# Causal attention: the values' product after every unit of scores, in banks of its own, summed by GpSimd

## The chip, the cores and the metric

The kernel runs on one core of a Trainium2 chip. The metric is device microseconds from start to end of one execution; the median of three runs of the kernel before is 4479.21 us (4477.16 to 4482.08). TensorE is called PE in the profile, VectorE DVE, ScalarE ACT, GpSimd POOL and SyncE SP.

## The reference, cut to what matters

The program is a chain of layers on x of 2 batches x 2048 tokens x 256 features in fp32: a mixture of experts, an attention without a mask, the experts again, a recurrent layer, a causal attention, the recurrent layer again. The change lies in the causal attention:

```python
q, k, v = shape(x @ w_q.T), shape(x @ w_k.T), shape(x @ w_v.T)   # 16 heads of 16
q, k = rotary(q), rotary(k)
q = q / sqrt(DIM_PER_HEAD)
scores = einsum('bhqd,bhkd->bhqk', q, k) + einsum('bhqd,qkd->bhqk', q, rel)
scores = where(causal, scores, NEG_INF)
attn = softmax(scores, axis=-1)
ctx = einsum('bhqk,bhkd->bhqd', attn, v) + einsum('bhqk,qkd->bhqd', attn, rel)
out = ctx.transpose(0, 2, 1, 3).reshape(B, L, MODEL_DIM) @ w_o.T
```

rel depends on the distance of query and key alone, clipped at 32. So only a band of 32 keys before each query needs more than a constant.

## The kernel before, in words

Both attentions work on groups: one batch, one block of 512 queries, four of the 16 heads (J = 4), each head's 16 features in a strip of 32 partitions. Scores are computed twice. The first pass (`largest`) puts queries on the partitions of a PSUM bank, and DVE takes each row's maximum. The maximum is transposed and added into a spare row of the queries (`subtract`), so that the second pass (`exponential`, in the causal attention `exp_band`, `exp_far` and `exp`) has keys on the partitions and maxima already subtracted; ACT writes its exponentials to SBUF (`pT`). The values' product (`weighted`) takes these, 128 keys at a time, four heads side by side in the columns of the array. One column of the values is ones, so that the sums for the division come with it. `divide` transposes the group's result and divides.

The order of PE, ACT and DVE is that of the program, written out by hand: the kernel counts steps, and each step has two units of score work. A unit is one block of 128 keys of the second pass for one group, and one piece of the first pass for a later group, four heads each. Other work (projections, rotation, positions, division, outputs) is entered under a step by `at(step, ...)`. The order of POOL and SP is left to a scheduler. Two fp32 matmul records of the profile make one product.

In the first attention (`attention0`, L606 on) half of a step's other work and then the values of the unit before follow each unit. Each key block's values go to a bank of their own; ACT copies it to SBUF (L673, L676), and POOL adds it to the group's result there (L677).

In the causal attention (`attention1`) a step's two units come one after the other, then all of the step's other work, then the values of both units of the step before. They accumulate in one PSUM bank per group, `z.acc[t]`, from the first key block to the positions' product (L1103), after which `z.take` copies it out (L553). Blocks on the diagonal take only the columns from q0 on. The band of a diagonal block comes by DMA from DRAM, is added to on POOL (L999), and is transposed into the scores' bank by PE (L1056, L1060). `rotate` (L885 to L894) makes rotated keys and queries: a copy on ACT, a shuffle on DVE, three or four operations on POOL. `by_position` (L923) is the first to read the rotated queries on PE. `ln_stats` puts the normalisation of later blocks on POOL (L100, L102, L113).

The pool of PSUM has eight banks for all of it. A causal group of query block qc has 4 (qc + 1) key blocks; over both batches there are 32 groups and 320 key blocks.

Of the kernel before, what the change touches and what calls it, by code (L numbers as in the profile page):

```python
# [10 lines left out]
F32 = mybir.dt.float32  # L11
AF = mybir.ActivationFunctionType
ALU = mybir.AluOpType
# [4 lines left out]
P = 128  # L18
# [7 lines left out]
TB = 512  # L26
NTB = NT // TB
CPB = TB // P
# [5 lines left out]
J = 4  # L34
# [8 lines left out]
def macaron_kernel(ctx: ExitStack, tc: tile.TileContext, t: dict, out: bass.AP):  # L43
    nc = tc.nc
# [26 lines left out]
    def bank():  # L71
        return psum.tile([P, TB], F32, name="s")
# [12 lines left out]
    class Norm:  # L85


        def __init__(self):
            self.mv, self.rstd, self.xn, self.xnT = {}, {}, {}, {}
# [42 lines left out]
    def rows(j):  # L132
        return slice(32 * j, 32 * j + 32)
# [351 lines left out]
    class Pieces:  # L485


        def __init__(self, s, name, norm, weights_o, bias):
            self.keep = pool(s, name + "_keep")
            self.wk = pool(s, name + "_wk", 2)  # L490
            self.norm, self.wo, self.bias = norm, weights_o, bias
            self.mnegs = []
            for n in range(2):
                m = self.keep.tile([P, CPB, J, 32], F32, name=f"mneg{n}")
                nc.gpsimd.memset(m, 0.0)
                self.mnegs.append(m)
            self.cn, self.cT, self.o, self.acc, self.pTs, self.q = ({} for _ in range(6))

        def ln_stats(self, b, qc):
            blk = b * SB + qc  # L500
# [46 lines left out]
                )  # L547
            nc.vector.tensor_tensor(self.q[t], self.q[t], pm, ALU.add)  # L548

        def take(self, t):  # L550

            self.o[t] = self.wk.tile([P, TB], F32, name="o")
            nc.scalar.copy(self.o[t], self.acc.pop(t))  # L553

        def divide(self, t, b, qc, g, own):
            if (b, qc) not in self.cn:
# [45 lines left out]
    def attention0(norm, tail, wq, wk_, wv, wo, bff):  # L602
# [7 lines left out]
        with ExitStack() as s:  # L610
            z = Pieces(s, "a0", norm, wo, bff)
            kpool = pool(s, "a0_k", side="right")
            vpool = pool(s, "a0_v", side="right")
            wk, q = z.wk, z.q
            groups = [(b, qc, g) for b in range(B) for qc in range(SB) for g in range(G)]
            NG = len(groups)
# [45 lines left out]
            def weighted(t, kb):  # L662
                b, qc, g = groups[t]
                pv = bank()
                for j in range(J):
                    h = (g % 2) * J + j
                    nc.tensor.matmul(  # L667
                        pv[rows(j), :], lhsT=v[b, g // 2][:, kb, ds(h * VW, 32)],
                        rhs=z.pTs.pop((t, kb, j)), start=True, stop=True,
                    )  # L670
                if kb == 0:
                    z.o[t] = wk.tile([P, TB], F32, name="o")
                    nc.scalar.copy(z.o[t], pv)  # L673
                else:
                    part = wk.tile([P, TB], F32, name="part", bufs=4)
                    nc.scalar.copy(part, pv)  # L676
                    nc.gpsimd.tensor_tensor(z.o[t], z.o[t], part, ALU.add)  # L677

            jobs = Jobs()
            at = jobs.at  # L680
# [29 lines left out]
            for step in range(min(jobs), max(jobs) + 1):  # L710
                todo = jobs.get(step, [])
                for n in range(2):
                    te, tm = (step - 9) // PER, step // PER
                    ke, um = ((step - 9) % PER) * 2 + n, (step % PER) * 2 + n
                    exps = 0 <= te < NG
# [144 lines left out]
    def attention1(norm, tail, w, relk, relv, kbias, dramp, skew):  # L860
# [4 lines left out]
        with ExitStack() as s:  # L865
            z = Pieces(s, "a1", norm, w["o"], None)
            wk, q = z.wk, z.q
            groups = []
# [3 lines left out]
            NG = len(groups)  # L872
            kT, v, mx, band, cos, sin, wb, wT, st, pd, lead = ({} for _ in range(11))
# [156 lines left out]
            def exp_far(t, kb, j):  # L1030
                b, qc, g = groups[t]
                qb = kb - qc * CPB
                ps = exp_bank(t, kb, j)
                k = kT[b, kb // CPB, g][rows(j), ts(kb % CPB, P)]
                q0 = 0
                if qb >= -1:
                    q0 = (qb + 1) * P
                    if q0 < TB:
                        nc.tensor.matmul(  # L1039
                            ps[0 : P - BAND, ds(q0, P)], lhsT=k[:, 0 : P - BAND],  # L1040
                            rhs=q[t][rows(j), ds(q0, P)], start=True, stop=True,
                            skip_group_check=True,
                        )
                    q0 += P
                if q0 < TB:
                    nc.tensor.matmul(  # L1046
                        ps[:, q0:], lhsT=k, rhs=q[t][rows(j), q0:], start=True, stop=True,
                        skip_group_check=True,
                    )

            def exp_band(t, kb, j):
                b, qc, g = groups[t]
                qb = kb - qc * CPB
                ps = exp_bank(t, kb, j)
                if qb >= 0:
                    nc.tensor.transpose(ps[:, ts(qb, P)], band[t][:, qb, j, BAND:], ident)  # L1056
                if qb + 1 < CPB:


                    nc.tensor.transpose(  # L1060
                        ps[:, ts(qb + 1, P)], lead[t][:, ds(((qb + 1) * J + j) * BW, P)], ident
                    )

            def exp(t, kb, j):
                q0 = max(0, kb - groups[t][1] * CPB) * P
                z.pTs[t, kb, j] = wk.tile([P, TB], F32, name="pT", bufs=16)
                nc.scalar.activation(z.pTs[t, kb, j][:, q0:], st.pop((t, kb, j))[:, q0:], AF.Exp)  # L1067

            def weighted(t, n, kb):
                b, qc, g = groups[t]  # L1070
                q0 = max(0, kb - qc * CPB) * P
                if n == 0:
                    z.acc[t] = bank()
                for j in range(J):
                    h = (g % 2) * J + j
                    nc.tensor.matmul(  # L1076
                        z.acc[t][rows(j), q0:],
                        lhsT=v[b, kb // CPB, g // 2][:, kb % CPB, ds(h * VW, 32)],
                        rhs=z.pTs.pop((t, kb, j))[:, q0:], start=n == 0, stop=False,
                        skip_group_check=True,  # L1080
                    )

            def positions_load(t):
                wb[t] = wk.tile([P, CPB, J * BAND], F32, name="s2", bufs=4)
# [15 lines left out]
                nc.vector.tensor_copy(wT[t], pw)  # L1100

            def positions(t):
                nc.tensor.matmul(  # L1103
                    z.acc[t], lhsT=relv, rhs=wT[t], start=False, stop=True, skip_group_check=True
                )


            Ms, Me, Es, Ee, Rs = [], [], [], [], []
            for n, (b, qc, g) in enumerate(groups):
                size = 2 * (qc + 1)  # L1110
                start = Me[-1] + 1 if n else 0
                if n > 1:
                    start = max(start, min(Ee[n - 2] + 1, Es[n - 2] + 5) + 2 - (size - 2))
                if n > 3:
                    start = max(start, Ee[n - 4] + 4)
                Ms.append(start)
                Me.append(start + size - 1)
                start = Me[-1] + 2
# [2 lines left out]
                Es.append(start)  # L1121
                Ee.append(start + size - 1)
                Rs.append(start + (3 if size == 2 else 4))
            largest_at, exp_at, weighted_at = Jobs(), Jobs(), Jobs()
            for n, (b, qc, g) in enumerate(groups):
                for i, piece in enumerate(pieces(qc)):
                    largest_at.at(Ms[n] + i // 2, None, n, *piece)
                for i, kb in enumerate(key_blocks(qc)):
                    exp_at.at(Es[n] + i // 2, None, n, i, kb)
                    weighted_at.at(Es[n] + i // 2 + 1, None, n, i, kb)  # L1130
            jobs = Jobs()
            at = jobs.at
            index = {x_: n for n, x_ in enumerate(groups)}
# [27 lines left out]

            for step, fn, *args in tail:
                at(Me[-1] + step, fn, *args)
            if True:
                for step in range(min(jobs), max(jobs) + 1):
                    exps = [a for _, a in exp_at.get(step, ())]
                    maxs = [a for _, a in largest_at.get(step, ())]
                    late = []
                    for n in range(2):
                        e = exps[n] if n < len(exps) else None  # L1170
                        m = maxs[n] if n < len(maxs) else None
                        qb = e[2] - groups[e[0]][1] * CPB if e is not None else -2
                        if -1 <= qb < CPB - 1:
                            for j in range(J):
                                exp_band(e[0], e[2], j)
                        for j in range(J):
                            if e is not None:
                                exp_far(e[0], e[2], j)
                                if qb == CPB - 1:
                                    late.append((e[0], e[2], j))  # L1180
                                else:
                                    exp(e[0], e[2], j)
                            if m is not None:
                                largest(*m, (j + 2) % J if e is not None else j)
                    for a_ in late:
                        exp_band(*a_)
                        exp(*a_)
                    jobs.run(step)
                    for _, a_ in weighted_at.get(step, ()):
                        weighted(*a_)  # L1190
                    for n in range(NG):
                        if step == max(Rs[n], Ee[n] + 1):
                            z.take(n)


    def load_all(stack, pool_, names):
# [210 lines left out]
```

## Time and profile before

| what | value |
|---|---|
| median of the runs | 4479.21 us |
| profiled execution, its own time | 4366.3 us |
| its span, first to last instruction | 4364.5 us |
| mean granted PE clock | 0.985 |
| causal attention, about | 2740 to 4180 us of the span |
| busy there (of 1440 us) | PE 1408.28, DVE 869.91, ACT 696.91, POOL 479.93 |
| first attention, about | 560 to 2090 us of the span |

The profile is of one execution, whose own time is below the median of the runs. A row of it names line, engine and operation; a matmul's duration is modelled, and several run at once in strips of the array, so that a busy PE isn't one at its full pace. The starts of matmuls show the pace.

### The profile page before, as it was taken

Reading aid. Unit: us, or ns where it says so; the run is one execution under the profiler, and the core shown is the slowest. Engines: PE = TensorE matmul, PEld = TensorE weight load, DVE = VectorE, ACT = ScalarE, POOL = GpSimd, SP = SyncE. Lnnn points to the kernel's source line nnn. Section 1 sums busy time; section 2 is a strip of 40 time slices with the busy share of each in tenths; the row PEclk is TensorE's granted clock in tenths of the full one; section 3 lists DMA queues with packets and bytes.
Section 4 is the critical chain, followed back from the end, with each engine's and each line's share of the span. In section 5 each row is a group of like instructions: output and inputs, shape, how many; then the busy total and the mean of one; then the engine's idle time right before and its main releaser. Section 6 shows DMA issues by size and latency. Waiting matters only on the chain.

```text
span 4364.5 us, 76072 instructions
## 1 busy us (share of the span) xinstructions
PE 4211.6 (96%) x28512; PEld 2106.7 (48%) x28512; DVE 2703.6 (62%) x6176; ACT 2398.1 (55%) x4835; POOL 1480.3 (34%) x1374
## 2 busy tenths in 40 slices
PE   7998999999999999999999897999999999999999
PEld 4664333333334333333356544565555555655545
DVE  6245787877766878888543343566666455666533
ACT  2331788877777888888623231344545534454532
POOL 4253333345332333333352311542222444322100
PEclk9999999999999999999999998999999999999999
DMA  7331000000000000000334200453212345222101
GB/s 250 122 116 42 1 1 1 1 1 1 1 1 2 1 1 1 1 1 8 110 131 126 84 10 22 105 117 81 66 44 49 73 100 114 58 61 45 44 21 39
DMA packets 355503, 224.33 MB, mean 51 GB/s; under 512 B 146496, under 2 KB 338496, under 8 KB 355136
## 3 DMA queue, kind: packets, MB, share of 16 engines
q1 hardware_dynamic: 342848, 185.89, 16.3%
q0 software_dynamic: 12288, 33.57, 2.4%
q8 instruction: 227, 3.72, 0.4%
q14 instruction: 140, 1.15, 0.1%
HBM read 114.29 MB, written 105.12 MB: 50 GB/s over the span
## 4 chain that ended last, share of the span: by engine, by line
PE 87%; DVE 6%; issue 2%; POOL 2%; DMA 1%; ACT 1%; SPq 0%; POOLq 0%; ACTq 0%; DVEq 0%
PE s L655 13%; PE s L667 11%; PE s L138 11%; PE s L643 10%; PE s L961 8%; PE s L1046 6%; PE s L358 6%; PE s L1076 6%; PE s L377 3%; PE s L585 1%; PE s L1056 1%; PE s L526 1%; PE s L1039 1%; PE s L1060 1%; DVE mx L969 1%
## 5 line engine op out<-in xcount | busy, mean ns | idle before, releaser
L647 DVE TENSOR_REDUCE mx<-s 128x1 f32<-128x512 f32 x2048 | 1271.5, 683 | 363.7 <-PE s L643 362.9
L660 ACT ACTIVATE pT<-s 128x512 f32<-128x512 f32 x2048 | 1064.2, 618 | 206.8 <-PE s L643 202.4
L655 PE MATMUL s<-q,kT 32*128 32x512 f32 x4096 | 1016.5, 616 | 6.3 <-DVE q L548 5.4
L643 PE MATMUL s<-kT,q 32*128 32x512 f32 x4096 | 1015.2, 618 | 6.8 <-DVE mx L647 5.5
L677 POOL TENSOR_TENSOR o<-o,part 128x512 f32<-128x512 f32 x480 | 608.4, 1268 | 1101.6 <-ACT part L676 1100.6
L1067 ACT ACTIVATE pT<-s 128x512 f32<-128x512 f32 (+3 forms) x1280 | 592.8, 545 | 485.6 <-PE s L1046 293.6
L655 PEld LDWEIGHTS s<-q,kT 32*128 32x128 f32 x4096 | 414.4, 184 | 471.9 <-DVE mx L647 310.5
L969 DVE TENSOR_REDUCE mx<-s 128x1 f32<-128x512 f32 (+1 forms) x768 | 466.5, 677 | 246.6 <-PE s L961 226.8
L667 PE MATMUL s<-pT,v 128*32 128x512 f32 x4096 | 549.9, 605 | 2.0 <-DVE mx L647 1.9
L643 PEld LDWEIGHTS s<-kT,q 32*128 32x128 f32 x4096 | 405.3, 184 | 138.0 <-ACT pT L660 71.6
L961 PE MATMUL s<-kT,q 32*128 32x160 f32 (+7 forms) x2240 | 398.1, 441 | 0.0
L676 ACT COPY part<-s 128x512 f32<-128x512 f32 x480 | 296.9, 619 | 79.3 <-PE s L667 78.8
L358 PE MATMUL s<-we,xT 128*128 x592 | 278.9, 593 | 0.6 <-ACT xT L353 0.6
L961 PE MATMUL s<-b,q 32*128 32x512 f32 (+7 forms) x1280 | 271.0, 528 | 6.2 <-POOL b L894 5.7
L1046 PE MATMUL s<-q,kT 32*128 32x512 f32 (+3 forms) x1152 | 265.4, 510 | 1.6 <-DVE s L1100 1.6
L1076 PE MATMUL s<-pT,v 128*32 128x512 f32 (+3 forms) x2560 | 266.7, 534 | 0.0
L999 POOL TENSOR_TENSOR band<-band,mneg 128x640 f32<-128x640 f32 x128 | 160.8, 1260 | 309.8 <-DVE mneg L995 309.4
L961 PEld LDWEIGHTS s<-kT,q 32*128 32x128 f32 x2240 | 226.1, 186 | 61.1 <-DVE mx L969 17.6
L1046 PE MATMUL s<-q,b 32*128 32x512 f32 (+3 forms) x896 | 248.4, 566 | 0.0
L667 PEld LDWEIGHTS s<-pT,v 128*32 128x32 f32 x4096 | 82.2, 108 | 337.6 <-ACT pT L660 282.0
L365 DVE TENSOR_TENSOR h<-sg,s 128x256 f32<-128x256 f32 x148 | 62.3, 421 | 288.5 <-ACT sg L363 288.5
L985 DVE CUSTOM_DVE_ANT_0 band<-s,band 128x160 f32<-128x160 f32 (+1 forms) x512 | 155.2, 315 | 95.4 <-PE s L1046 51.6
(209 smaller groups left out, 5535.2 us busy)
## 6 DMA issues: line engine op xcount, KB each, us to landing
band<-skew SPq DMA_DIRECT2D x32, 1280.0 KB
pd<-band SPq DMA_DIRECT2D x32, 1280.0 KB, 8.3
xs<-places SPq DMA_DIRECT2D x148, 128.0 KB, 2.1
results<-y SPq DMA_DIRECT2D x148, 128.0 KB, 2.0
places<-zero SPq DMA_DIRECT2D x2, 4736.0 KB, 23.9
we<-in_we SPq DMA_DIRECT2D x12, 768.0 KB, 6.5
skew<-s SPq DMA_DIRECT2D x32, 256.0 KB, 3.0
s<-pd SPq DMA_DIRECT2D x32, 256.0 KB, 3.0
```

Source lines behind the costliest of these rows:

```text
L358: nc.tensor.matmul(pu, lhsT=xT[i][:, ts(kc, P)], rhs=w[:, kc, ds(val[i], 2 * D)], start=kc == 0, stop=kc == 1,)
L643: nc.tensor.matmul(ps, lhsT=q[t][rows(j), ts(qb, P)], rhs=kT[b, g][rows(j), ts(kc, TB)], start=True, stop=True,)
L647: nc.vector.tensor_reduce(mx[t][:, qb * J + j, kc : kc + 1], ps, AX.X, ALU.max)
L655: nc.tensor.matmul(st, lhsT=kT[b, g][rows(j), ts(kb, P)], rhs=q[t][rows(j), :], start=True, stop=True,)
L660: nc.scalar.activation(z.pTs[t, kb, j], st, AF.Exp)
L667: nc.tensor.matmul(pv[rows(j), :], lhsT=v[b, g // 2][:, kb, ds(h * VW, 32)], rhs=z.pTs.pop((t, kb, j)), start=True, stop=True,)
L677: nc.gpsimd.tensor_tensor(z.o[t], z.o[t], part, ALU.add)
L961: nc.tensor.matmul(ps[:, ds(cols, n)], lhsT=lhsT, rhs=kT[b, c, g][rows(j), ds(k0, n)], start=True, stop=True,)
L969: nc.vector.tensor_reduce(m[:, c : c + 1], ps[:, 0:n], AX.X, ALU.max)
L1046: nc.tensor.matmul(ps[:, q0:], lhsT=k, rhs=q[t][rows(j), q0:], start=True, stop=True, skip_group_check=True,)
L1067: nc.scalar.activation(z.pTs[t, kb, j][:, q0:], st.pop((t, kb, j))[:, q0:], AF.Exp)
L1076: nc.tensor.matmul(z.acc[t][rows(j), q0:], lhsT=v[b, kb // CPB, g // 2][:, kb % CPB, ds(h * VW, 32)], rhs=z.pTs.pop((t, kb, j))[:, q0:], s ...
```

## The change

The values of the causal attention follow each unit: half of the step's other work, then the values of the unit before. Each key block's go to a bank of their own, are copied to SBUF by ACT, and are added by POOL to the group's result. The positions' product gets a bank, a copy and a sum too. The accumulating bank and `z.take` go. The method `gather`, which does copy and sum, now serves both attentions. The buffers of `pT` in the causal attention fall from 16 to 12.

```diff
-        def take(self, t):
-            self.o[t] = self.wk.tile([P, TB], F32, name="o")
-            nc.scalar.copy(self.o[t], self.acc.pop(t))
+        def gather(self, t, pv, q0=0):
+            if t not in self.o:
+                self.o[t] = self.wk.tile([P, TB], F32, name="o")
+                nc.scalar.copy(self.o[t], pv)
+                return
+            part = self.wk.tile([P, TB], F32, name="part", bufs=4)
+            nc.scalar.copy(part[:, q0:], pv[:, q0:])
+            o = self.o[t][:, q0:]
+            nc.gpsimd.tensor_tensor(o, o, part[:, q0:], ALU.add)
...
-                z.pTs[t, kb, j] = wk.tile([P, TB], F32, name="pT", bufs=16)
+                z.pTs[t, kb, j] = wk.tile([P, TB], F32, name="pT", bufs=12)
...
-            def weighted(t, n, kb):
+            def weighted(t, kb):
                 b, qc, g = groups[t]
                 q0 = max(0, kb - qc * CPB) * P
-                if n == 0:
-                    z.acc[t] = bank()
+                pv = bank()
                 for j in range(J):
                     h = (g % 2) * J + j
                     nc.tensor.matmul(
-                        z.acc[t][rows(j), q0:],
+                        pv[rows(j), q0:],
                         lhsT=v[b, kb // CPB, g // 2][:, kb % CPB, ds(h * VW, 32)],
-                        rhs=z.pTs.pop((t, kb, j))[:, q0:], start=n == 0, stop=False,
-                        skip_group_check=True,
-                    )
+                        rhs=z.pTs.pop((t, kb, j))[:, q0:], start=True, stop=True,
+                    )
+                z.gather(t, pv, q0)
...
             def positions(t):
-                nc.tensor.matmul(
-                    z.acc[t], lhsT=relv, rhs=wT[t], start=False, stop=True, skip_group_check=True
-                )
+                pv = bank()
+                nc.tensor.matmul(pv, lhsT=relv, rhs=wT[t], start=True, stop=True)
+                z.gather(t, pv)
...
+            ready = []
+            for step in range(min(jobs), max(jobs) + 1):
                 exps = [a for _, a in exp_at.get(step, ())]
                 maxs = [a for _, a in largest_at.get(step, ())]
-                late = []
+                todo = jobs.get(step, [])
                 for n in range(2):
                     e = exps[n] if n < len(exps) else None
                     m = maxs[n] if n < len(maxs) else None
...
                     for j in range(J):
                         if e is not None:
                             exp_far(*e, j)
+                            if qb < CPB - 1:
+                                exp(*e, j)
                         if m is not None:
                             largest(*m, (j + 2) % J if e is not None else j)
+                    if qb == CPB - 1:
+                        for j in range(J):
+                            exp_band(*e, j)
+                            exp(*e, j)
+                    for fn, args in todo[n * (len(todo) + 1) // 2 :][: (len(todo) + 1 - n) // 2]:
+                        fn(*args)
+                    for a_ in ready:
                         weighted(*a_)
+                    ready = [e] if e is not None else []
-                jobs.run(step)
-                for _, a_ in weighted_at.get(step, ()):
-                    weighted(*a_)
-                for n in range(NG):
-                    if step == max(Rs[n], Ee[n] + 1):
-                        z.take(n)
```

For the last block of the diagonal (qb = CPB - 1) band and exponentials came at the step's end (`late`), and now come at the end of their unit.

More of the change, by code (lines that the diff above doesn't have):

```diff
@@ L496, in __init__ @@
                 self.mnegs.append(m)
-            self.cn, self.cT, self.o, self.acc, self.pTs, self.q = ({} for _ in range(6))
+            self.cn, self.cT, self.o, self.pTs, self.q = ({} for _ in range(5))
         def ln_stats(self, b, qc):
@@ L670, in weighted @@
                     )
[L671 to L677, printed above, removed]
+                z.gather(t, pv)
             jobs = Jobs()
@@ L1102, in positions @@
             def positions(t):
-                nc.tensor.matmul(
-                    z.acc[t], lhsT=relv, rhs=wT[t], start=False, stop=True, skip_group_check=True
-                )
+                pv = bank()
+                nc.tensor.matmul(pv, lhsT=relv, rhs=wT[t], start=True, stop=True)
+                z.gather(t, pv)
             Ms, Me, Es, Ee, Rs = [], [], [], [], []
@@ L1123, in attention1 @@
                 Rs.append(start + (3 if size == 2 else 4))
-            largest_at, exp_at, weighted_at = Jobs(), Jobs(), Jobs()
+            largest_at, exp_at = Jobs(), Jobs()
             for n, (b, qc, g) in enumerate(groups):
@@ L1128, in attention1 @@
                 for i, kb in enumerate(key_blocks(qc)):
-                    exp_at.at(Es[n] + i // 2, None, n, i, kb)
-                    weighted_at.at(Es[n] + i // 2 + 1, None, n, i, kb)
+                    exp_at.at(Es[n] + i // 2, None, n, kb)
             jobs = Jobs()
@@ L1163, in attention1 @@
                 at(Me[-1] + step, fn, *args)
[L1164 to L1167, printed above, removed]
-                    late = []
[L1169 to L1175, printed above, removed]
-                        for j in range(J):
[L1177 to L1187, printed above, removed]
-                    jobs.run(step)
-                    for _, a_ in weighted_at.get(step, ()):
@@ new lines, in attention1 @@
+            ready = []
+            for step in range(min(jobs), max(jobs) + 1):
+                exps = [a for _, a in exp_at.get(step, ())]
+                maxs = [a for _, a in largest_at.get(step, ())]
+                todo = jobs.get(step, [])
+                for n in range(2):
+                    e = exps[n] if n < len(exps) else None
+                    m = maxs[n] if n < len(maxs) else None
+                    qb = e[1] - groups[e[0]][1] * CPB if e is not None else -2
+                    if -1 <= qb < CPB - 1:
+                        for j in range(J):
+                            exp_band(*e, j)
+                    for j in range(J):
+                        if e is not None:
+                            exp_far(*e, j)
+                            if qb < CPB - 1:
+                                exp(*e, j)
+                        if m is not None:
+                            largest(*m, (j + 2) % J if e is not None else j)
+                    if qb == CPB - 1:
+                        for j in range(J):
+                            exp_band(*e, j)
+                            exp(*e, j)
+                    for fn, args in todo[n * (len(todo) + 1) // 2 :][: (len(todo) + 1 - n) // 2]:
+                        fn(*args)
+                    for a_ in ready:
```

## The prediction

> **What bounds the kernel now.** I read the page's totals and its chain first. TensorE (PE) carries both, so I looked at how PE's time is made up where the change acts: in the timeline of the causal attention (2740 to 4180 us of the span), beside the same work in the first attention (560 to 2090 us), which already puts its values behind every unit.
>
> ```profile
> PE 4211.6 (96%) x28512; PEld 2106.7 (48%) x28512; DVE 2703.6 (62%) x6176; ACT 2398.1 (55%) x4835; POOL 1480.3 (34%) x1374
> PE 87%; DVE 6%; issue 2%; POOL 2%; DMA 1%; ACT 1%; SPq 0%; POOLq 0%; ACTq 0%; DVEq 0%
> ```
>
> A busy PE is not a PE at its pace. First attention, PE's timeline (start, duration, line, records):
>
> ```profile
> 1501.76 1.06 PE L667 MATMUL s<-pT,v 128*32 128x512 f32 x8
> 1502.76 0.69 PE L655 MATMUL s<-q,kT 32*128 32x512 f32 x1
> ...
> 1503.30 0.59 PE L655 MATMUL s<-q,kT 32*128 32x512 f32 x1
> ...
> 1503.72 0.59 PE L655 MATMUL s<-q,kT 32*128 32x512 f32 x1
> ...
> 1504.69 1.07 PE L667 MATMUL s<-pT,v 128*32 128x512 f32 x8
> ```
>
> Four records start every 0.43 us, 0.1075 each. A unit is 16 records of scores, 1.93 us from their start to the next values (1.72 at that pace, 0.21 lost), and 8 of values, 1.00 us (0.86, 0.14 lost): 2.93 us.
>
> Causal attention, one step of two units with both score passes and no other work but four transposes; PE's timeline, then VectorE's (DVE) and ScalarE's (ACT):
>
> ```profile
> 3992.29 1.92 PE L1076 MATMUL s<-pT,v 128*32 128x512 f32 x16
> 3994.14 0.69 PE L1046 MATMUL s<-q,kT 32*128 32x512 f32 x1
> ...
> 3999.02 0.66 PE L544 MATMUL s<-ident,mneg 128*128 128x128 f32 x4
> ```
>
> ```profile
> 3995.34 4.91 DVE L969 TENSOR_REDUCE mx<-s 128x1 f32<-128x512 f32 x8 [1.34 <-PE s L961]
> ```
>
> ```profile
> 3995.36 2.56 ACT L1067 ACTIVATE pT<-s 128x512 f32<-128x512 f32 x5 [2.49 <-PE s L961]
> 3998.09 1.64 ACT L1067 ACTIVATE pT<-s 128x512 f32<-128x512 f32 x3 [0.17 <-PE s L1046]
> ```
>
> The 32 score records take 4.88 us where the pace gives 3.44. DVE stands idle 1.34 us during the values, then does its eight maxima without a gap in 4.91 us. Sixteen score banks arrive in a row, seven are free (one of the eight holds the group's sum from its first value to its last), and PE gets the next when a maximum or an exponential lets one go. While PE does values, DVE and ACT have nothing. Two such units in the first attention would take 2 x 2.93 = 5.86 us; here 4.88 + 1.85 = 6.73. So the stage is bound in turn by DVE and by PE.
>
> Over the stage, score runs take 882 us of PE time against 543 at the pace, values 257 against 234, all else 288 against 262 (starts of matmuls in the trace, runs cut by line).
>
> **What the skill says.** "TensorEngine Tiling (Array Packing)", PSUM Bottleneck: after a fourfold tiling the emptying of PSUM may become the limit; the 4.91 us above agrees. The same page, Key Properties: a change of tiling mode drains the engine; that fits the 0.21 and 0.14 us. "SBUF — State Buffer", Who interferes with whom: a tensor_reduce does not contend with GpSimd; the trace agrees, since maxima take 683 ns in the first attention beside GpSimd's sums and 677 in the causal one without. "PSUM — Partial Sum Buffer", The four PSUM rules: GpSimd can't reach PSUM, hence the copy.
>
> **The change, part by part.** The build's order has as many PE, DVE and DMA instructions as before (16247, 6115, 567), and 320 more on ACT and on POOL each.
>
> *Values behind every unit.* A gain. PE's need of a step is its records at the pace, plus 0.35 us for each of two units, plus 0.17 for each run of other work (288 - 262 over 146 runs). A group of the last query block, at 4001.5 to 4066.3 us: its eight steps take 7.71, 9.94, 7.42, 10.12, 8.05, 5.70, 6.74 and 9.15, together 64.8. For example, the 7.42 has 24 full score records (2.58), 8 of 128 columns (0.21), 8 transposes (0.86) and values worth 1.50: 5.16, so 5.86 with the 0.70. Streaming of all eight is 48.2; with 16 x 0.35 and 1.0 for other work, 54.8. Does another engine come last then? DVE has 41.9 there, ACT 34.4 + 8.2 for its copies, POOL 14.3 + 18.4. Only one step has: that of 5.70, where ACT has 4.03 and two copies of 0.55, 5.1 against PE's 4.2. That makes 55.7, a gain of 9.1; eight such groups, 73. A group of the third block (3060.3 to 3112.6, six steps): 52.3 now, streaming 38.7, plus 12 x 0.35 and 0.8: 43.7, gain 8.6; eight, 69. For the eight pairs of short groups (58 us each, streaming 41) I count only 3 us each, 24: there the maxima over the diagonal fill DVE (18.0 of 25.1 us from 2802.1) and PE waits up to 2.7 us for the queries' subtraction. Sum 166.
>
> *One more change of mode per step*: two fills where one was; it is in the 0.35.
>
> *Copies on ACT.* 288 parts of values and 32 of positions; the 32 copies of the group's sum (L553) become those of the first key block. A full one costs 0.52 to 0.62 (2.56 / 5 back to back; 619 ns is the mean row of the first attention's copies): 224 full and 96 narrower, about 155 us, hidden behind PE except where ACT has all the work: the steps after a batch's last maximum (4123 to 4160, 3446 to 3461), eight exponentials and two copies, 5.2 us where 4.7 are taken now. About twelve steps, 6 us lost. A copy waits for its values with the next unit's exponentials queued behind; those come later from PE anyway.
>
> *Sums on POOL.* 224 of 512 columns at 1268 ns (the row of L677) and 96 of 384, 256, 128: 346 us, making POOL 480 + 346 of some 1300. Off the path if the queries' rotation, the band's subtraction and the last sum before a group's division stay ahead of PE. In the trace a rotated query lies ready 5.6 to 14.6 us before the product that reads it (0.1 and 1.1 for the first two groups, where nothing is to sum); two or three sums in front cost 2.5 to 3.8. The division comes a step after the last sum, some 5 us for a copy and a sum of 1.9 together.
>
> *Banks and buffers.* The eighth bank comes free, and a part of values holds one for 1.6 us. 12 in place of 16 exponentials: three units live at once, as in the first attention. The positions' product gets a bank, a copy and a sum, counted above.
>
> *Unevenness.* The steps' sums hide lags inside a unit: on the diagonal DVE has 5.31 / 2 = 2.65 us per unit against 2.8 of PE, so its cover is gone. Bounds: nothing, or half of the gain. I take off 35 us, 1.1 a group.
>
> Sum: 166 - 6 - 35 = 125 us. Against the profiled execution, 4366.3 us (its span 4364.5): 4241. The runs' median is 112.9 above that; I carry this over unchanged: 4479.2 - 125 = 4354.
>
> **Rivals.**
> - *The whole of it*: nothing held back, also not in the short groups. Score runs 543 + 0.21 x 320, values 234 + 0.14 x 320, the rest 300: 1190 against 1426, 236 less, so 4243. For it: the first attention does just this. Against: the diagonal's DVE load.
> - *Half of it*: ACT or DVE lags in every unit with a diagonal, 60 us gained: 4419. For it: four band transposes take four banks at once, before any can be let go.
> - *PE was the bound* (slower): were score runs long for PE's own sake, the change would only add a switch of modes, 160 steps x 0.35 = 56 us: 4535. Against it: eight maxima without a gap, exactly as long as the run.
> - *POOL comes late* (slower): POOL keeps its queue in order, and two layer norms in a row hold it for 12 us (L113, 4 x 1.2, with L102, twice); meanwhile the four parts' buffers fill, ACT waits with a copy, and exponentials queue behind. This decides from 125 / 32 = 3.9 us of PE stall per group; at 5 us, 160 lost: 4514. For it: POOL's 37 busy of 65 us around 3583. Against: the slack above.
>
> **Chances and range.** Forecast (gain 80 to 170) 0.57; the whole 0.13; half or a little 0.15; POOL late 0.08; PE the bound 0.04; no measurable change (within 0.2%, about what a measurement of this kernel can tell) 0.03. Faster 0.85, same 0.03, slower 0.12. Range 4290 to 4440: it takes in most of the forecast's and the half's, and leaves out the slower cases and the best half of the whole. Given faster, 4280 to 4425.
>
> **What would show it.** Right: in the full step maxima come in fours with values between, two units take about 5.9 us in place of 6.7; the stage 2740 to 4180 shrinks by some 125 us with PE, DVE and DMA counts the same; the first attention stays. Wrong: PE idle before L1076 or the division with POOL's sum or ACT's copy as releaser; ACT waiting for a part's buffer; score runs of eight banks still above 2.4 us; or the first attention changed.

## The result and the profile after

The changed kernel takes 4446.08 us (4436.4 to 4446.38) against 4478.3 before: 0.9921 of it, 95% interval 0.9904 to 0.9939. It is faster by 32 us where 125 were forecast, and lies just above the forecast's range.

The runs come from several chips. The kernel before takes some 4479 us on some of them and 4367 on the others; its profile is from one of the second kind, that of the changed kernel from one of the first. The difference lies ahead of the causal attention, which begins near 2820 us of the span on the first kind and near 2706 on the second; over the causal attention itself the granted clock is alike (0.99 before, 0.98 after). So I compare ratios, and the causal attention's own length: from the first projected query on PE to the last output product, by the starts of matmuls in the trace, called the stage below. It goes with the times: 1465.8 us before and 1430.9 after, 34.9 less.

The page of the changed kernel: PE's totals and three groups.

```profile
PE 4178.2 (94%) x28512; PEld 2000.7 (45%) x28512; DVE 2711.3 (61%) x6176; ACT 2543.0 (57%) x5155; POOL 1825.1 (41%) x1694
...
L560 POOL TENSOR_TENSOR o<-o,part 128x512 f32<-128x512 f32 (+3 forms) x800 | 962.4, 1203 | 1418.9 <-ACT part L558 1414.6
...
L1068 ACT ACTIVATE pT<-s 128x512 f32<-128x512 f32 (+3 forms) x1280 | 589.9, 546 | 269.6 <-PE s L1047 115.2
...
L558 ACT COPY part<-s 128x512 f32<-128x512 f32 (+3 forms) x800 | 466.6, 585 | 220.6 <-PE s L1076 101.9
```

Counts are as forecast, and ACT and POOL got about what was counted: ACT has 145 us more than before (2398.1) for the 155 forecast, POOL 345 (1480.3) for 346. Ahead of its exponentials (L1067 before) ACT stood idle 486 us before and 270 now. Ahead of its copies of parts it stands idle 221 us now, in both attentions; the first attention alone had 79 before.

PE's timeline of two units, the second one with bands:

```profile
4087.90 1.06 PE L1076 MATMUL s<-pT,v 128*32 128x512 f32 x8
4088.90 0.69 PE L1047 MATMUL s<-q,kT 32*128 32x512 f32 x1
...
4090.83 1.06 PE L1076 MATMUL s<-pT,v 128*32 128x512 f32 x8
4091.82 0.33 PE L1057 MATMUL s<-ident,band 128*128 128x128 f32 x1
...
4092.84 0.34 PE L1040 MATMUL s<-q,kT 32*96 32x128 f32 x1
4092.86 0.69 PE L962 MATMUL s<-b,q 32*128 32x512 f32 x1
...
4093.39 0.61 PE L962 MATMUL s<-b,q 32*128 32x512 f32 x2
4093.82 0.27 PE L1040 MATMUL s<-q,kT 32*96 32x128 f32 x1
...
4094.90 1.07 PE L1076 MATMUL s<-pT,v 128*32 128x512 f32 x8
```

and DVE's beside it:

```profile
4090.10 2.48 DVE L970 TENSOR_REDUCE mx<-s 128x1 f32<-128x512 f32 x4 [0.60 <-PE s L962]
4094.02 2.48 DVE L970 TENSOR_REDUCE mx<-s 128x1 f32<-128x512 f32 x4 [1.44 <-PE s L962]
```

The first unit is what was forecast: scores 1.93 us, values 0.99, maxima in fours. The second isn't: its scores take 3.08 us, from 4091.82 to 4094.90. In it short products (L1040, 128 columns) and long ones (L962, 512) take turns in the strips of the array. PE begins the next four products 0.43 us after the start of the last long records (4093.39 to 4093.82), while the strips with the short ones stand empty.

The stage by sections, from one maximum's transposition to that of a later group ("short": the groups of the first two query blocks; "qc2", "qc3": of the third and fourth; the start, 45 to 50 us, is left out):

| us | before | after | work unsplit | no sums | divide later | order only | seven banks |
|---|---|---|---|---|---|---|---|
| short, batch 0 | 192.1 | 203.9 | 195.2 | 199.7 | 190.6 | 202.0 | 212.2 |
| qc2, batch 0 | 206.6 | 189.8 | 189.9 | 189.6 | 191.5 | 213.1 | 216.2 |
| qc3, batch 0 | 262.4 | 247.2 | 247.3 | 243.7 | 249.0 | 280.0 | 288.1 |
| short, batch 1 | 254.3 | 267.0 | 252.8 | 261.8 | 246.5 | 271.2 | 277.9 |
| qc2, batch 1 | 206.3 | 189.8 | 189.9 | 189.6 | 191.7 | 213.4 | 216.2 |
| qc3, batch 1 | 246.9 | 230.9 | 228.1 | 230.9 | 228.9 | 268.3 | 272.1 |
| last | 51.6 | 54.6 | 53.6 | 52.0 | 52.8 | 50.9 | 55.1 |
| stage | 1465.8 | 1430.9 | 1402.2 | 1415.2 | 1396.5 | 1546.7 | 1587.6 |

The long groups gained 64.5 us, the short ones lost 24.5. By kind of work, as PE time above the streaming (0.1075 us for a record of 512 columns in a strip or of 128 in the whole array): scores 343.6 before and 253.8 after, values 22.6 and 53.0, other work 42.5 (148 runs) and 67.0 (223 runs). A run is a stretch of one kind of work on PE, up to the start of the next.

### The profile page after: what moved, and what is told of

It reads as the page before. It is cut to its first block, busy times and chain, and to the rows that moved or that the text cites. A ratio compares the mean times of both kernels' runs of the same rounds, so it can differ in the third digit from the quotient of the medians.

```text
span 4444.6 us, 77325 instructions
## 1 busy us (share of the span) xinstructions
PE 4178.2 (94%) x28512; PEld 2000.7 (45%) x28512; DVE 2711.3 (61%) x6176; ACT 2543.0 (57%) x5155; POOL 1825.1 (41%) x1694
## 4 chain that ended last, share of the span: by engine, by line
PE 82%; DVE 7%; POOL 3%; issue 3%; another core or an unknown queue 2%; DMA 2%; ACT 1%; SPq 0%; POOLq 0%; ACTq 0%; DVEq 0%
PE s L662 12%; PE s L674 11%; PE s L138 11%; PE s L650 10%; PE s L1076 5%; PE s L962 5%; PE s L358 5%; PE s L1047 5%; PE s L377 3%; PE s L592 1%; PE s L527 1%; PE s L1057 1%; PE s L1040 1%; PE s L1061 1%
## 5 line engine op out<-in xcount | busy, mean ns | idle before, releaser
L560 POOL TENSOR_TENSOR o<-o,part 128x512 f32<-128x512 f32 (+3 forms) x800 | 962.4, 1203 | 1418.9 <-ACT part L558 1414.6
L558 ACT COPY part<-s 128x512 f32<-128x512 f32 (+3 forms) x800 | 466.6, 585 | 220.6 <-PE s L1076 101.9
L650 PEld LDWEIGHTS s<-kT,q 32*128 32x128 f32 x4096 | 405.4, 184 | 139.3 <-ACT pT L667 71.1
L358 PE MATMUL s<-we,xT 128*128 x592 | 289.1, 612 | 37.8 <-ACT xT L353 19.7
L962 PE MATMUL s<-kT,q 32*128 32x512 f32 (+7 forms) x2240 | 320.1, 437 | 2.8 <-ACT part L558 2.8
L1076 PE MATMUL s<-pT,v 128*32 128x512 f32 (+3 forms) x2560 | 306.6, 545 | 0.9 <-DVE mx L970 0.4
L403 POOL DMA_INDIRECT yg<-results,at x128 | 125.0, 977 | 314.9 <-PE s L358 104.9
L962 PE MATMUL s<-b,q 32*128 32x512 f32 (+7 forms) x1280 | 240.2, 528 | 5.7 <-POOL b L895 5.7
L1047 PE MATMUL s<-q,kT 32*128 32x512 f32 (+3 forms) x1152 | 233.8, 516 | 0.0
L1047 PE MATMUL s<-q,b 32*128 32x512 f32 (+3 forms) x896 | 195.6, 575 | 0.0
```

The costliest lines, as they stand in the source:

```text
L358: nc.tensor.matmul(pu, lhsT=xT[i][:, ts(kc, P)], rhs=w[:, kc, ds(val[i], 2 * D)], start=kc == 0, stop=kc == 1,)
L560: nc.gpsimd.tensor_tensor(o, o, part[:, q0:], ALU.add)
L650: nc.tensor.matmul(ps, lhsT=q[t][rows(j), ts(qb, P)], rhs=kT[b, g][rows(j), ts(kc, TB)], start=True, stop=True,)
L962: nc.tensor.matmul(ps[:, ds(cols, n)], lhsT=lhsT, rhs=kT[b, c, g][rows(j), ds(k0, n)], start=True, stop=True,)
L1047: nc.tensor.matmul(ps[:, q0:], lhsT=k, rhs=q[t][rows(j), q0:], start=True, stop=True, skip_group_check=True,)
L1076: nc.tensor.matmul(pv[rows(j), q0:], lhsT=v[b, kb // CPB, g // 2][:, kb % CPB, ds(h * VW, 32)], rhs=z.pTs.pop((t, kb, j))[:, q0:], start=T ...
```

## Experiments

### Which half of the change does it

`order_only`: after every unit as in the changed kernel, but added up in the group's bank.

```diff
-                pv = bank()
+                first = t not in acc
+                if first:
+                    acc[t] = bank()
...
-                        rhs=z.pTs.pop((t, kb, j))[:, q0:], start=True, stop=True,
+                        rhs=z.pTs.pop((t, kb, j))[:, q0:], start=first, stop=False,
```

> The order alone: values after every unit as in the changed kernel, but added up in one bank per group as before, copied out once; no parts, no sums on GpSimd. Causal attention from the first projected query to the last output product: 1466 us before, 1431 us changed. If the order brings the gain and the copies, sums and banks only cost (theory A): the short groups' loss of some 26 us goes, 1395 to 1410 us here, 4410 to 4425 us in all. If the freed bank brings it (theory B): as before, 1460 to 1470, 4475 to 4480. If PE's own switches eat what is missing from the forecast (theory C): as the changed kernel or little below, 1420 to 1435, 4435 to 4450.

`banks_only`: own banks, copies and sums, with two units' values at the step's end.

```diff
-                    for a_ in ready:
-                        weighted(*a_)
-                    ready = [e] if e is not None else []
+                jobs.run(step)
+                for a_ in ready + exps[:1]:
+                    weighted(*a_)
+                ready = exps[1:]
```

> The banks alone: own banks, copies on ScalarE and sums on GpSimd as in the changed kernel, but both units of a step first, then all other work, then the values of two units (one unit earlier than before, since 12 buffers of exponentials hold no more). Theory A: nothing is gained by it and the sums cost, 4480 to 4510 us. Theory B: as the changed kernel, near 4446.

The order alone came out as no theory had it, *slower* than before: 1.0186 (1.0169 to 1.0203), the stage 1546.7. The banks alone gain nothing, 1.0003 (0.9994 to 1.0012), as the first theory said; the stage was 1473.4 us in its trace, which is of the slowest of twelve executions. Only both together gain. In `order_only` a full unit's 16 score records take 2.86 us on average, in the changed kernel 2.07. Either the held bank is missed, or PE's adding into one bank is slow.

`seven_banks`: the changed kernel with one bank held throughout.

```diff
+            held = bank()
+            nc.vector.memset(held[:, 0:2], 0.0)
             ready = []
```

> The changed kernel, unaltered but for one PSUM bank taken at the start of the causal attention's steps and let go after them, so that seven are left. If the order alone was slow because a unit's eight score products need eight free banks: full units of 16 score records take 2.8 to 2.9 us in place of 2.07, and the stage some 0.8 us more for about 150 units, 4540 to 4570 us in all. If accumulating in one bank was slow for another reason (PE adding into a bank it has just written): no loss beyond 20 us, 4446 to 4466.

1.0276 (1.0258 to 1.0293), the stage 1587.6, 157 us above the changed kernel's. Full units take 2.90 us. PE's timeline of one, and the lines of ACT and DVE beside it:

```profile
4086.32 0.69 PE L1047 MATMUL s<-q,kT 32*128 32x512 f32 x1
...
4088.13 1.12 PE L962 MATMUL s<-kT,q 32*128 32x512 f32 x2
4089.18 0.43 PE L1076 MATMUL s<-pT,v 128*32 128x128 f32 x8
```

```profile
4087.48 2.06 ACT L1068 ACTIVATE pT<-s 128x512 f32<-128x512 f32 x4 [0.38 <-PE s L962]
4087.52 2.48 DVE L970 TENSOR_REDUCE mx<-s 128x1 f32<-128x512 f32 x4 [2.11 <-PE s L962]
```

A unit has eight score products. Seven find a bank at once. The eighth begins at 4088.13, 1.81 us after the first, when a bank comes back: the first results are read some 1.2 us after the first start (4086.32 to 4087.48), and a maximum or an exponential takes 0.6. It then runs almost alone with its two records, where eight banks let it run beside others. Here each unit has a bank of its own for its values, nothing is added up in a bank, and the full units are as slow as in `order_only` (2.90 and 2.86). So the missing bank is enough to explain them, and the own banks weren't the price of the order but its condition. The stage is longer than in `order_only`; there the values take no further bank, here theirs come out of the seven too.

### What held the steps before

`half_maxima`: the kernel before, with cheaper maxima, taken over half of the columns, so that what is subtracted isn't the true maximum.

```diff
-                    nc.vector.tensor_reduce(m[:, c : c + 1], ps[:, 0:n], AX.X, ALU.max)
+                    nc.vector.tensor_reduce(m[:, c : c + 1], ps[:, 0 : n // 2], AX.X, ALU.max)
```

> The kernel before, with the far maxima of the causal attention taken over the first half of each product's columns (so what is subtracted is not the true maximum). VectorE then needs 0.35 us for one in place of 0.61. If it set the pace of the steps with two score passes: score runs of 32 records fall from 4.88 us to the 4.2 to 4.4 of ScalarE's eight exponentials; 40 to 60 us less, 4420 to 4440. If PE's own pace did: no change, 4470 to 4485.

0.9906 (0.9889 to 0.9923), 42 us less, as expected if DVE held PE up. But not where I had read it. The score runs with bands fell (40 score records and eight transposes, 29 of them: 5.91 to 5.30 us); the full ones of 32 records stayed at 4.87. Timelines of DVE and ACT in such a step (scores from 3837.11 to 3841.98):

```profile
3838.31 1.29 DVE L969 TENSOR_REDUCE mx<-s 128x1 f32<-128x256 f32 x3 [2.79 <-PE s L961]
...
3840.13 2.38 DVE L969 TENSOR_REDUCE mx<-s 128x1 f32<-128x256 f32 x5 [0.53 <-PE s L1046]
```

```profile
3838.32 2.56 ACT L1067 ACTIVATE pT<-s 128x512 f32<-128x512 f32 x5 [3.36 <-PE s L961]
...
3841.05 1.58 ACT L1067 ACTIVATE pT<-s 128x512 f32<-128x512 f32 x3 [0.17 <-PE s L1046]
```

DVE now has gaps, ACT none but 0.17 us, and the run is as long as before. PE's timelines show why. Products of the first pass in the full step of the prediction (scores from 3994.14), then here:

```profile
3996.01 0.69 PE L961 MATMUL s<-b,q 32*128 32x512 f32 x1
...
3996.50 0.69 PE L961 MATMUL s<-b,q 32*128 32x512 f32 x2
...
3996.99 0.69 PE L961 MATMUL s<-b,q 32*128 32x512 f32 x2
```

```profile
3838.97 0.69 PE L961 MATMUL s<-b,q 32*128 32x512 f32 x1
...
3839.46 0.69 PE L961 MATMUL s<-b,q 32*128 32x512 f32 x2
...
3839.95 0.69 PE L961 MATMUL s<-b,q 32*128 32x512 f32 x2
```

They start 1.87, 2.36 and 2.85 us after the first score there, and 1.86, 2.35 and 2.84 here; in both traces each starts 0.05 us after an exponential ended. So the full step ran at the pace of ACT's exponentials already before the change, and that eight maxima without a gap lasted just as long as the run was a coincidence. DVE did hold the steps with bands. A run with cheaper exponentials, which would test this further, wasn't made.

### The other work

`work_unsplit`: all of it after the second unit. `work_after_first`: all after the first.

```diff
-                    for fn, args in todo[n * (len(todo) + 1) // 2 :][: (len(todo) + 1 - n) // 2]:
+                    for fn, args in todo if n == 1 else ():
```

> The changed kernel with all of a step's other work after its second unit, not half after each: 148 runs of other work in place of 223, at 0.30 us lost per run. If that loss is the runs' own: 22 us less, 4424. If the split work is also what lets DVE catch up after the first unit: no gain or a loss, 4446 to 4470.

> The changed kernel with all of a step's other work after its first unit. If the split costs by the number of runs of other work (148 in place of 223, 0.30 us each): the stage as with all of it after the second unit, 1397 to 1408 us, ratio to the kernel before near 0.986. If it matters that the work stands at the step's end, where its inputs have had longest: as the changed kernel or worse, stage 1425 to 1450, ratio 0.991 to 0.997.

After the second: 0.9861 (0.9844 to 0.9877), stage 1402.2. After the first: 0.9891 (0.9874 to 0.9907), stage 1422.6. Both have 148 runs of other work. Their loss above streaming is 46.4 and 57.5 us, 67.0 with the split. So the number of runs isn't all: of the 28.7 us that the first gains, the second gains 8.3. The rest is the place, and it lies in the short groups: 448.0 us with the work last, 464.8 with it first, 470.9 split, 446.4 before. Waits of PE with the work first (in total, how often, the longest):

```profile
PE s L569 <- POOL o L560: 12.7, 5, 3.4
...
PE s L1057 <- DVE b L573: 6.7, 10, 2.4
PE s L1061 <- ACT s L888: 6.5, 6, 1.8
```

The division's wait for the last sum doesn't make the difference: it is 14.3 us with the work last (below). The other two are not among the waits with the work last. As I read them, the bands' transpositions, which open a unit, wait there for the reader of a bank that a division or a projection has just filled. But with the work last PE waits 10.0 us for the queries' subtraction instead. So the waits don't add up to the 20 us between the two runs, and why the place matters stays open.

### GpSimd's sums

`no_sums`: parts are copied and not added, so that the result holds the first key block alone. `divide_later`: the work unsplit, and the division one step later.

```diff
-            o = self.o[t][:, q0:]
-            nc.gpsimd.tensor_tensor(o, o, part[:, q0:], ALU.add)
+            if add:
+                o = self.o[t][:, q0:]
+                nc.gpsimd.tensor_tensor(o, o, part[:, q0:], ALU.add)
```

```diff
-                at(end + 1, z.divide, n, b, qc, g, False)
+                at(end + 2, z.divide, n, b, qc, g, False)
```

> The changed kernel without GpSimd's sums in the causal attention: parts are copied out and left, so the result there holds the first key block alone. If late sums hold PE up in the short groups (14 us over both batches and the division waits of 25 us in the trace): 20 to 30 us less, 4416 to 4426. If not: within 8 us of 4446.

> The run with the other work after the second unit (stage 1402 us, ratio 0.986), with each group's division and outputs one step later. If the 16 us that PE waits there for GpSimd's last sums at the division, and the 16 us that the run without sums gained, are this one wait: stage 1385 to 1392 us, ratio 0.982 to 0.984. If PE then waits for something else: stage 1397 to 1410, ratio as it was.

Without the sums the ratio is 0.9893 (0.9877 to 0.991), the stage 15.7 us shorter than the changed kernel's (12 us by the ratios): short of the 20 expected, 9.4 of it in the short groups. The division later: 0.9836 (0.9819 to 0.9852), the stage 5.7 us shorter than with the work unsplit, not 10 to 17. The waits of PE suggest why. Unsplit:

```profile
PE s L569 <- POOL o L560: 14.3, 5, 4.1
PE s L1040 <- DVE q L549: 10.0, 5, 2.8
```

With the division later:

```profile
PE s L1040 <- DVE q L549: 15.6, 9, 2.6
...
PE s L569 <- POOL o L560: 2.2, 1, 2.2
```

The wait for the last sum is gone (14.3 to 2.2), and half of it comes back as a wait for the queries' subtraction, next in the chain. The short groups gain 10.9 us in all, the long ones lose 6. This is the fastest version with true maxima: faster than before by 1.6%, where the changed kernel is by 0.8%.

### The units at the diagonal

`apart`: unsplit, and where lengths differ, four heads' products of the one kind, then four of the other. `apart_maxima_first` has the maxima first where there is no band.

```diff
+                    apart = e is not None and m is not None and (qb >= -1 or m[2] is None)
                     for j in range(J):
...
-                        if m is not None:
+                        if m is not None and not apart:
                             largest(*m, (j + 2) % J if e is not None else j)
+                    for j in range(J) if apart else ():
+                        largest(*m, j)
```

> The run with the other work unsplit (4416 us, stage 1402), with one more edit: where a unit's exponential and maximum products differ in length (blocks at the diagonal), all four heads' products of the second pass come first, then all four of the first pass, instead of in turn. If strips of the array lie idle there because PE starts its records in order and a long one stands in front of a short one: 41 units with bands go from 3.05 to 2.55 us and 44 with narrow maxima from 2.12 to 1.8, stage 1365 to 1375, 4380 to 4390 in all. If those units are held by VectorE or ScalarE: no gain or a loss, 4410 to 4440.

> As the run before, but in units without a band (far exponentials beside diagonal maxima) the maxima come first. VectorE has 2.65 us of work in such a unit against 2.0 to 2.6 of ScalarE, so if its late start matters there: 5 to 15 us less than with the exponentials first. If the array's order is all that matters: the same within 5 us.

Both lose against the unsplit run: 0.9918 (0.9901 to 0.9934) and 0.9933 (0.9917 to 0.995), stages 1434.1 and 1436.3; where the maxima stand in units without a band changes the stage by 2 us only. Yet the units with bands did get shorter, 3.05 to 2.73 us; full units got longer, 2.09 to 2.45. Two more runs take DVE's load away from the unsplit kernel and from this one, with the edit of `half_maxima`:

> The run with the other work after the second unit (stage 1402 us), with far maxima over half of the columns only (so what is subtracted is not the true maximum). If the units with bands (3.05 us of scores) are held by the order in which PE starts its records, not by VectorE: they stay at 2.95 or more, and the stage loses 10 us at most, 1392 to 1402. If VectorE still holds them: 2.5 us, and a stage of 1375 to 1385.

> The run that did the two kinds of products one after the other at the diagonal (stage 1434 us), with far maxima over half of the columns. If it lost because the maxima came late in the unit and VectorE carried that into the next (full units 2.45 in place of 2.09): those return to 2.05 to 2.15, units with bands stand at 2.5 to 2.6, and the stage is 1370 to 1390. If it lost for another reason: full units stay above 2.3, stage above 1410.

Unsplit with cheap maxima: units with bands stay at 3.04 us, so DVE doesn't hold them; full units fall from 2.09 to 1.94, so there DVE still did, a little. The stage is 1375.0 (ratio 0.979, 0.9774 to 0.9806), 27 us less where at most 10 were expected: 12 in the full units, 7 in the units of the diagonal's last block, 6 in four steps where two units' scores run together. Apart with cheap maxima: full units return to 2.09, units with bands stand at 2.72, a little above the 2.5 to 2.6 expected, the stage at 1386.0 (0.9816, 0.9799 to 0.9832). So the strips do lie idle for the sake of the order; setting it right brings the maxima late, and DVE carries them into the next unit.

## Why the prediction was wrong

- *The main mechanism held.* Alternate feeding shortened the full units as forecast: 1.93 us and 0.99 in the timeline, 2.07 on average over 82 such runs, where half of a full step's scores was 2.44. Counts, the copies' and the sums' loads came about as counted. Carrying the 112.9 us over to the runs' median was right: the stage fell by 34.9 us, the time by 32.
- *"PE's need of a step is its records at the pace" failed.* It divides all records evenly over four strips. Where products of different length take turns they can't be. Units with a band and full maxima took 3.19 us on average (45 of them) where the rule gives 2.24 + 0.21; those with narrow maxima beside far exponentials 2.17 (49) where it gives 1.46 + 0.21. That is 33 and 25 us, the largest piece of the shortfall by kind of work. In the first kind `unsplit_half_maxima` shows that DVE isn't the cause, and `apart` that 0.32 us of it is the order. Another 0.16 us lies between the bands' transpositions and the first product in strips, in 43 of the 45 units (4091.82 to 4092.84 in the timeline, 1.02 us for 0.86 of streaming): a second change of kind inside a unit, which the rule's 0.21 doesn't count. In the other two units PE waited 3 us there, which makes 0.13 of the average. Some 0.1 us of the first kind is open. Of the second kind 39 of the 49 take 2.02 or 2.03 us, one waits and takes 6.09. `apart` didn't shorten them on average (2.12 to 2.23); with the maxima first eight of 44 fell to 1.61 to 1.66, near what the rule gives, and others rose to 2.6. So the order has a part there too, and how large a part is open.
- *The number of runs of other work* was taken as unchanged, and halving each step's work made 223 of 148. Ahead of the first maximum's transposition PE waits for its first inputs in both kernels; without that part the loss is 0.18 us a run before (144 runs), near the 0.17 forecast, and 0.23 after (218 runs): 23 us more, where I had put nothing. Where the work stands had no price either. `work_unsplit` gives back 28.7 us.
- *The short groups* were to gain 24 us and lost 24.5. 23 of these come back with the work unsplit; the sums' part is 9.4. The long groups gained 64.5 of the 101 us that are left of their 142 when the 35 and the 6 are taken off.
- *What held the steps before* was misread. The prediction took DVE for the bound of the full step; the starts of products show ACT there, and `half_maxima` left the step as long as it was. Emptying banks was the limit, but not by DVE's 4.91 us. DVE held the steps with bands, and of the unsplit kernel's stage it still holds 27 us.
- *Rivals.* "Half of it" was nearest, with 60 us, but the lag that it named isn't what the runs show: of the units with bands DVE holds only those of the diagonal's last block, and ACT's part was not tested. "POOL comes late" came true in small, not by the layer norms it named: 15.7 us without the sums, of which the division's wait for the last sum is 11.3 in the changed kernel's waits. "PE was the bound" is refuted by the changed kernel itself, whose full units take 2.07 us for the records that took 2.44.
- *"The eighth bank comes free"* got no number. It is worth 157 us of the stage: without it the same change loses 122 us against the kernel before.
- *Unevenness*, 35 us taken off for DVE's maxima over the diagonal, had the right sign. Its reason isn't shown: no run made those maxima cheaper, and that 39 of the 49 units with them beside far exponentials take the same time speaks against it. The last steps' 6 us for copies were hardly needed: the last section took 3.0 us more than before, and 0.4 more in `no_sums`, so most of it is the sums'. The range's upper end took "half" as the worst of the faster cases, and left nothing below it.

## What to carry to other kernels

A step's need on a tiled TensorE isn't the sum of its columns over four where lengths differ. Counting products that run together by the longest of them comes nearer: an estimate for the units with bands, from the figures above, is 0.86 for the transpositions, twice 0.86 for two rounds of long products, 0.21 and 0.16, together 2.95 us, against 2.45 by the sum and 3.19 measured. Setting products of equal length together shortened such units, but the kernel got slower, because the maxima then came late. Before interleaving for balance, count the banks that one unit takes at once; one too few turned this gain into a loss larger than the gain. Work that is moved into gaps makes more runs and may stand in a worse place: one place gave back 28.7 us here and the other 8.3, so try more than one.

## What was not expected of the hardware

Eight concurrent score products of two records each take 2.07 us with eight banks free and 2.90 with seven. In the full units shown, of four kernels, the first results are read 1.2 us after the first record starts; with 0.6 us for the reader that makes a bank's turn 1.8 us. Accumulating into one PSUM bank, unit after unit, isn't slower in itself: values take 0.88 us on average in `order_only`, and 0.90 in the changed kernel. Going from transpositions in the whole array to products in strips took 0.16 us above streaming, in 43 of 45 units.
